# A four-image scan, attention and expert kernel: other VectorE work is put between each tick's product and scan

## The chip, the cores and the metric

The kernel runs on one core of a Trainium2 chip. A core has five engines that run side by side and each take their instructions in the order in which the program issues them: TensorE (PE, matmuls into PSUM), VectorE (DVE), ScalarE (ACT), GpSimd (POOL) and SyncE (SP, which here only issues DMAs). They wait for one another through semaphores. The metric is the device time of one execution in microseconds (us). Before the change it is 3908.64 us, the median of three runs (3907.09 to 3909.1).

## The reference, cut to what matters

There are four images of 384 channels and 32 x 32 pixels, so 1024 positions, in fp32. Layer 0 is a selective scan in four directions behind a group norm, layer 1 is causal attention and a mixture of four experts.

```python
# layer 0: x = x + gelu(layernorm(scan(groupnorm(x))))
def _gn(v, G=32, eps=1e-5):
    g = v.reshape(B_, G, C_ // G, H_, W_)
    m = jnp.mean(g, axis=(2, 3, 4), keepdims=True)
    s = jnp.var(g, axis=(2, 3, 4), keepdims=True)
    return ((g - m) / jnp.sqrt(s + eps)).reshape(v.shape)
...
def step(h, inp):                       # for every direction k, channel d, state n (16)
    dtt, ut, bt, ct = inp
    dA = jnp.exp(dtt[..., None] * A)
    h = h * dA + (dtt * ut)[..., None] * bt[:, :, None, :]
    y = jnp.einsum('bkdn,bkn->bkd', h, ct)
    return (h, y)
...
# layer 1
t = t + softmax(causal(q k^T)) v        # q, k, v from layernorm(t)
scores = jnp.einsum('bsd,de->bse', x, gate_w) + gate_b
probs = jax.nn.softmax(scores, axis=-1)
topk_vals, topk_idx = jax.lax.top_k(probs, TOP_K)       # 2 of 4
masked = probs * mask
masked = masked / (jnp.sum(masked, axis=-1, keepdims=True) + 1e-09)
h = jax.nn.gelu(jnp.einsum('bsd,edh->ebsh', x, w1) + b1)
y = jnp.einsum('ebsh,ehd->ebsd', h, w2) + b2
out = jnp.einsum('bse,ebsd->bsd', masked, y)
```

## The kernel before

The program is written out by hand in ticks (the `while` loop from L1158, with the tick in `clock`). There are 768 scan units: 4 images x 3 channel blocks `m` x 4 directions `k` x 4 state groups `q` x 4 channel groups `j`; each has 128 partitions (32 channels x 4 states) and 1024 positions. Tick t issues, in this order:

1. `decay(t + 2)` on ACT: da = exp(dt x a) (L505), three buffers;
2. what was deferred to this tick (`due`);
3. `front(t)` on DVE: v = du x B (L512), into PSUM, one buffer; both inputs are in SBUF;
4. `back(t - 1)` on POOL: the product h x C (L525), made to wait for this tick's v (`order`), both inputs in SBUF;
5. what was deferred to the inner place of this tick (`inner`), and the generators that parked themselves (`unpark`);
6. `middle(t)` on DVE: the scan (L518);
7. after every fourth unit `row(t - 2)` on PE, which sums the states into y (L550); then the DMAs for later ticks (`fetch`);
8. one step of the preparation of the next image, and `go_on`: the side generators, then the main work in line (`waiting`).

So DVE work that is issued in place 2 stands ahead of v, in place 5 between v and the scan, and in place 8 behind the scan, ahead of the next tick's v. A generator yields `"wait", n` to sleep n ticks, `"pe", x` to charge x us of PE to its budget, and `"inner", 0` to be taken up in place 5 of the next tick. The budget is `pace[0]` per tick: PACE_A = 4.4 in an attention, PACE_E = 3.3 in the experts.

What goes on beside the scans:

- `preparation(b)` loads image b, does its group norm (L297 to L338), the projections (`project_x`, `project_dt`), and writes dt and du = dt x u to DRAM, from where they are spread over the states. `project_dt` multiplies du in place 8 (L395), in the tick in which it takes a slot for it.
- `evict` (L566) collects y of an image; `finish(b)` does the layernorm, gelu, and the addition of x (L707, place 2). Then `behind(b)` runs `attention` and `experts`. `layernorm` subtracts (L601) and scales (L649) in place 5 and takes the reciprocal (L633) in place 8. It serves three callers.
- In attention, `softmax` (L777) stands in place 5 and `normalise` (L791), one tick later, in place 2. `gates` (L868) is a chain of small DVE operations in place 8, with a tick between its parts.
- `experts` runs 8 steps (2 halves x 4 experts); each has 12 groups `ph` (L1027), 6 groups `fy` (L1052) and three `out_` on DVE in place 5 (L1061, L1064). Behind the last expert of a half, `store` (L997) sends the result out.

Eight shared SBUF slots (`slots`) hold weights, du, dt, squares and softmax rows in turn; four PSUM banks (`banks`) are shared likewise. One large buffer, tag `a0`, holds the normed input of an attention (`axn`, L715) and then the second input and the accumulator of the same image's experts (`fx1`, L1081): the next image's axn cannot be written until the last store of the experts has been read out.

## Time and profile before

| what | us |
|---|---|
| median of three runs | 3908.64 |
| the profiled execution | 3911.65 |
| its span in the profile | 3909.9 |
| PE busy, of the span | 3382.8 (87%) |
| DVE busy | 3096.5 (79%) |
| ACT busy | 1887.9 (48%) |
| POOL busy | 1809.5 (46%) |
| start of the first v | 49.26 |
| start of the last scan | 3235.30 |
| first matmul of the last attention (L737) | 3302.51 |

The profile is one execution, taken by the hardware. A group line of it reads: line, engine, operation, output<-inputs, shapes and count | busy us in total, mean ns of one | idle time of the engine just before them, and what ended most of it. A line of waits reads: who <- for whom: us in total, times, longest. A line in order of time reads: start, duration, engine, line, operation. An instruction that is held up after it has started shows as a long one, not as idle time. A busy PE is modelled, and is not PE at its peak. The engines in the order of their load in the stretch of the scans are DVE and PE, close together; behind the last scan DVE and POOL have little to do.

### The profile page before, as it was taken

Reading aid. Unit: us, or ns where it says so; the run is one execution under the profiler, and the core shown is the slowest. Engines: PE = TensorE matmul, PEld = TensorE weight load, DVE = VectorE, ACT = ScalarE, POOL = GpSimd, SP = SyncE. Lnnn points to the kernel's source line nnn. Section 1 sums busy time; section 2 is a strip of 40 time slices with the busy share of each in tenths; the row PEclk is TensorE's granted clock in tenths of the full one; section 3 lists DMA queues with packets and bytes.
Section 4 is the critical chain, followed back from the end, with each engine's and each line's share of the span. In section 5 each row is a group of like instructions: output and inputs, shape, how many; then the busy total and the mean of one; then the engine's idle time right before and its main releaser. Section 6 shows DMA issues by size and latency. Waiting matters only on the chain.

```text
span 3909.9 us, 32087 instructions
## 1 busy us (share of the span) xinstructions
PE 3382.8 (87%) x10623; PEld 1389.4 (36%) x10623; DVE 3096.5 (79%) x2258; ACT 1887.9 (48%) x1996; POOL 1809.5 (46%) x776
## 2 busy tenths in 40 slices
PE   4554655659899999978999999799999998999999
PEld 1100100015433334435433343354334334644444
DVE  6999999998999999979999899989999993110000
ACT  5442543446656656546656545555455453322121
POOL 2665666654555556535555566455566661000000
PEclk7665666679899999989999999899999999999999
DMA  5554545453576667535666666426566651132321
GB/s 192 203 183 148 197 147 188 162 189 127 191 239 208 236 223 241 184 112 190 223 211 214 212 218 213 162 105 227 179 214 213 222 187 44 61 90 82 96 82 55
DMA packets 406087, 671.85 MB, mean 172 GB/s; under 512 B 33265, under 2 KB 280353, under 8 KB 405921
## 3 DMA queue, kind: packets, MB, share of 16 engines
q1 hardware_dynamic: 399712, 669.41, 50.5%
q8 instruction: 84, 1.38, 0.1%
q10 hardware_dynamic: 6208, 0.39, 0.1%
q14 instruction: 83, 0.67, 0.1%
HBM read 597.75 MB, written 71.96 MB: 171 GB/s over the span
## 4 chain that ended last, share of the span: by engine, by line
DVE 49%; PE 38%; issue 5%; ACT 4%; DMA 2%; POOL 1%; DVEq 1%; SPq 0%; POOLq 0%; ACTq 0%
DVE h L518 29%; DVE v L512 15%; PE ph L1027 13%; PE fy L1052 12%; PE y L550 3%; PE ss L766 2%; PE pq L737 2%; PE pv L748 2%; PE po L832 1%; ACT da L505 1%; DVE fy L1061 1%; ACT ht L1016 1%; PE pxd L350 1%; DMA du<-dts 1%; DVE du L395 1%
## 5 line engine op out<-in xcount | busy, mean ns | idle before, releaser
L525 POOL TENSOR_TENSOR h<-h,bc 128x1024 f32<-128x1024 f32 x768 | 1808.4, 2355 | 1430.0 <-DVE v L512 1278.1
L518 DVE TENSOR_TENSOR_SCAN h<-da,v 128x1024 f32<-128x1024 f32 x768 | 1755.5, 2286 | 86.1 <-DVE v L512 1.5
L505 ACT ACTIVATE da<-dt,a 128x1024 f32<-128x1024 f32 x768 | 878.0, 1147 | 1232.3 <-DVE h L518 1171.7
L1027 PE MATMUL ph<-fx,w 128*128 128x512 f32 x2304 | 1027.5, 602 | 9.4 <-ACT ht L1012 3.8
L1052 PE MATMUL fy<-ht,w 128*128 128x512 f32 x2304 | 1015.8, 598 | 2.4 <-ACT dt L387 0.9
L512 DVE TENSOR_TENSOR v<-du,bc 128x1024 f32<-128x1024 f32 x768 | 947.2, 1233 | 38.5 <-DMA du<-dts 16.4
L550 PE MATMUL y<-h,sel 128*32 128x512 f32 x3072 | 703.7, 713 | 309.5 <-POOL h L525 295.3
L1027 PEld LDWEIGHTS ph<-fx,w 128*128 128x128 f32 x2304 | 434.8, 192 | 588.9 <-issue 530.7
L1052 PEld LDWEIGHTS fy<-ht,w 128*128 128x128 f32 x2304 | 435.5, 191 | 570.5 <-issue 551.7
L1012 ACT ACTIVATE ht<-ph,b1s 128x512 f32<-128x512 f32 x384 | 257.6, 679 | 453.0 <-PE ph L1027 452.5
L550 PEld LDWEIGHTS y<-h,sel 128*32 128x32 f32 x3072 | 118.3, 118 | 831.7 <-POOL h L525 579.2
L1061 DVE SCALAR_TENSOR_TENSOR fy<-fy,b2s,tw 128x512 f32<-128x512 f32 x96 | 72.3, 754 | 424.1 <-PE fy L1052 424.1
L1016 ACT ACTIVATE ht<-ht 128x3072 f32<-128x3072 f32 x64 | 176.9, 2764 | 0.8
L505 ACT ACT_TABLE_LOAD x110 | 141.1, 1283 | 14.4 <-DMA dt<-dts 12.5
L766 PE MATMUL ss<-axn,qt 128*128 128x512 f32 (+3 forms) x288 | 105.3, 512 | 7.4 <-ACT yb L844 5.8
L832 PE MATMUL po<-pt,vt 128*128 128x256 f32 x480 | 103.6, 363 | 6.7 <-ACT pt L728 6.7
L832 PEld LDWEIGHTS po<-pt,vt 128*128 128x128 f32 x480 | 91.9, 193 | 21.7 <-ACT pt L728 9.2
L780 DVE TENSOR_REDUCE nb<-ss 128x1 f32<-128x512 f32 (+3 forms) x48 | 26.2, 554 | 82.8 <-PE ss L771 64.6
L381 PE MATMUL pdt<-xd,wdt 12*128 12x512 f32 x184 | 61.5, 690 | 34.4 <-ACT xd L354 26.5
L766 PEld LDWEIGHTS ss<-axn,qt 128*128 128x128 f32 x288 | 52.3, 199 | 53.3 <-issue 36.5
L1064 DVE TENSOR_TENSOR fx<-fx,fy 128x512 f32<-128x512 f32 x96 | 65.9, 687 | 3.3
L1016 ACT ACT_TABLE_LOAD x50 | 64.2, 1283 | 0.9
(183 smaller groups left out, 1406.5 us busy)
## 6 DMA issues: line engine op xcount, KB each, us to landing
bc<-rows SPq DMA_DIRECT2D x384, 512.0 KB, 4.7
w<-in_w SPq DMA_DIRECT2D x384, 384.0 KB, 6.0
dt<-dts SPq DMA_DIRECT2D x192, 512.0 KB, 4.0
du<-dts SPq DMA_DIRECT2D x192, 512.0 KB, 6.1
dts<-dt SPq DMA_DIRECT2D x48, 512.0 KB, 4.9
dts<-du SPq DMA_DIRECT2D x48, 512.0 KB, 4.6
fx<-t2d SPq DMA_DIRECT2D x12, 768.0 KB, 6.0
tw<-mkd SPq DMA_DIRECT2D x32, 256.0 KB, 5.7
```

The lines of the kernel that those rows point to most:

```text
L505: nc.scalar.activation(u["da"], spread["dt4", n], AF.Exp, scale=a4[:, g, u["q"] : u["q"] + 1])
L512: return nc.vector.tensor_tensor(u["v"], spread["du4", n], spread["bc", n][:, 0, :], ALU.mult)
L518: nc.vector.tensor_tensor_scan(u["h"][:, ::step], u["da"][:, ::step], u["v"][:, ::step], 0.0, op0=ALU.mult, op1=ALU.add,)
L525: product = nc.gpsimd.tensor_tensor(h, h, spread["bc", n][:, 1, :], ALU.mult)
L550: nc.tensor.matmul(y, sel, h, start=first, stop=last, tile_position=(0, jj * DJ))
L766: nc.tensor.matmul(ps[:, : e - o], qt[:, c, i * P : (i + 1) * P], xn[:, c, o:e], start=(c == 0), stop=(c == M - 1 and e <= i * P),)
L832: nc.tensor.matmul(pv[:, o:], vt[:, j, m * P : (m + 1) * P], pts[step][j // 4][:, j % 4, o:], start=False, stop=(j == nj - 1),)
L1012: nc.scalar.activation(ht[:, f, :], ps, AF.Identity, bias=bias)
L1016: nc.scalar.activation(ht, ht, AF.Gelu)
L1027: nc.tensor.matmul(ps, tiles[n][:, c, (f % 2) * P : (f % 2 + 1) * P], xns[h][:, c, :], start=(c == 0), stop=(c == M - 1),)
L1052: nc.tensor.matmul(pss[m], tiles[n][:, f, :], hts[fh][:, f, :], start=(fh == 0 and f == 0), stop=(fh == 1 and f == FH - 1),)
L1061: nc.vector.scalar_tensor_tensor(ps, ps, b2s[:, e, m : m + 1], tw, ALU.add, ALU.mult)
```

## The change

What it does, part by part:

- `unpark` comes ahead of `back`, and `"inner", n` now parks for n ticks more. `both` holds the DVE instruction for which the product waits: v, or, in a tick that has one, the du multiplication or the addition of x.
- du, the addition of x, `normalise`, the reciprocal of `layernorm` and the parts of `gates` go to place 5. Where ACT makes the input (the reciprocal, the second part of `gates`, the first du of a pair), one tick later. The two stores of du move accordingly.
- The ranks of the four gates are counted by comparing all with all in four operations of 128 x 64 and a sum, instead of in a loop; `lower` breaks ties by index. It is set by four memsets at the start.
- The group norm of images 1 to 3 takes its sums on ACT (Identity and Square with an accumulator), into one slot.
- `layernorm` can make its output buffer late: in attention axn is taken only when the image before is stored.
- PACE_E is 3.4; the store of an expert's half comes 3 ticks behind the last `fy` instead of 4.

```diff
@@ -41,7 +41,7 @@
 BANKS = 4
 SLOTS = 8
 PACE_A = 4.4
-PACE_E = 3.3
+PACE_E = 3.4
 @with_exitstack
@@ -95,6 +95,7 @@
     clock = [-100]
     due = {}
     inner = {}
+    both = []
     def defer(ticks, f, where=due):
         where.setdefault(clock[0] + ticks, []).append(f)
@@ -200,6 +201,11 @@
     a4 = const.tile([P, K * NG, NQ], F32, tag="a4", name="a4")
     sel = const.tile([P, DJ], F32, tag="sel", name="sel")
+    lower = const.tile([P, E, E], F32, tag="lower", name="lower")
+    nc.vector.memset(lower, 0.0)
+    for e in range(1, E):
+        nc.vector.memset(lower[:, e, :e], 1.0)
     dump = const.tile([P, 1], F32, tag="dump", name="dump")
     nc.scalar.activation(a_raw, a_raw, AF.Exp)
     nc.scalar.activation(dump, eps, AF.Sqrt)
@@ -297,7 +303,25 @@
     def groupnorm(b, u):
         st = sm.tile([P, M, NH, 6], F32, tag="gn_st", name=f"gn_st_{b}")
         mv = sm.tile([P, M, 2], F32, tag="gn_mv", name=f"gn_mv_{b}")
-        for m in range(M):
+        mean_c = sm.tile([P, M], F32, tag="gn_mc", name=f"gn_mc_{b}")
+        if b > 0:
+            var_c = sm.tile([P, M], F32, tag="gn_vc", name=f"gn_vc_{b}")
+            sq = yield from slots.take(f"gn_sq_{b}", P, L)
+            for m in range(M):
+                nc.scalar.activation(
+                    sq, u[m], AF.Identity, scale=-1.0 / L, accum_out=mean_c[:, m : m + 1]
+                )
+                yield "wait", 1
+            for m in range(M):
+                nc.scalar.activation(
+                    sq, u[m], AF.Square, bias=mean_c[:, m : m + 1], accum_out=var_c[:, m : m + 1]
+                )
+                yield "wait", 1
+            slots.give(f"gn_sq_{b}")
+            yield "inner", 0
+            nc.vector.tensor_scalar_mul(mean_c, mean_c, -1.0)
+            nc.vector.tensor_scalar_mul(var_c, var_c, 1.0 / L)
+        for m in range(M) if b == 0 else ():
             for h in range(NH):
                 nc.vector.bn_stats(st[:, m, h, :], u[m][:, h * 512 : (h + 1) * 512])
             nc.vector.bn_aggr(mv[:, m, :], st[:, m].rearrange("p h s -> p (h s)"))
@@ -306,8 +330,8 @@
             yield "wait", 1
         if b == 0:
             nc.vector.tensor_scalar_mul(gback, pgb[:NGRP, :C], float(C // NGRP))
-        mean_c = sm.tile([P, M], F32, tag="gn_mc", name=f"gn_mc_{b}")
-        nc.vector.tensor_copy(mean_c, mv[:, :, 0])
+            var_c = mv[:, :, 1]
+            nc.vector.tensor_copy(mean_c, mv[:, :, 0])
         yield "wait", 1
         mean = sm.tile([P, M], F32, tag="gn_mean", name=f"gn_mean_{b}")
         ps = yield from over_group(mean_c, f"mean_{b}")
@@ -316,7 +340,7 @@
         dev = sm.tile([P, M], F32, tag="gn_dev", name=f"gn_dev_{b}")
         nc.vector.tensor_sub(dev, mean_c, mean)
         nc.vector.tensor_mul(dev, dev, dev)
-        nc.vector.tensor_add(dev, dev, mv[:, :, 1])
+        nc.vector.tensor_add(dev, dev, var_c)
         yield "wait", 1
         rstd = sm.tile([P, M], F32, tag="gn_rstd", name=f"gn_rstd_{b}")
         ps = yield from over_group(dev, f"var_{b}")
@@ -388,14 +412,22 @@
                     dts[i][:, bass.ts(h, 512)], pss[i], AF.Softplus, bias=dtb[:, k, m : m + 1]
                 )
                 banks.give(f"pdt_{b}_{k}_{m}_{h}")
-        yield "wait", 1
+        def store(k, du):
+            nc.sync.dma_start(dts_d[b, k][1, m * P : (m + 1) * P, :], du)
+            slots.give(f"dt_{b}_{k}_{m}", f"du_{b}_{k}_{m}")
+        last = ()
         for i, k in enumerate(ks):
             nc.sync.dma_start(dts_d[b, k][0, m * P : (m + 1) * P, :], dts[i])
             du = yield from slots.take(f"du_{b}_{k}_{m}", P, L)
-            nc.vector.tensor_mul(du, dts[i], v)
-            yield "wait", 1
-            nc.sync.dma_start(dts_d[b, k][1, m * P : (m + 1) * P, :], du)
-            slots.give(f"dt_{b}_{k}_{m}", f"du_{b}_{k}_{m}")
+            yield "inner", 1 - i
+            both[:] = [nc.vector.tensor_mul(du, dts[i], v)]
+            if last:
+                store(*last)
+            last = k, du
+        yield "wait", 1
+        store(*last)
         if pair == 1:
             slots.give(f"ut_{b}_{m}")
@@ -577,14 +609,14 @@
             waiting.append(behind(b))
-    def layernorm(dst, src, name, lag):
-        width = dst.shape[2]
+    def layernorm(dst, src, name, lag, b=0, into=None):
+        width = src.shape[2]
         n = width // 512
         mus = []
         for h in range(n):
@@ -595,6 +627,11 @@
                 )
             mus.append(mu)
             yield "pe", 2.6
+        if into is not None:
+            while b > 0 and b - 1 not in stored:
+                yield "wait", 1
+            dst = into()
         yield "inner", 0
         for h in range(n):
             s = bass.ts(h, 512)
@@ -629,7 +666,7 @@
             rs, var[:, : n * P].rearrange("p (h t) -> p h t", t=P), AF.Sqrt, bias=eps
         )
         banks.give(f"var_{name}")
-        yield "wait", 1
+        yield "inner", 1
         nc.vector.reciprocal(rs, rs)
         yield "wait", lag
         backs = []
@@ -651,6 +688,7 @@
                 ALU.mult,
             )
             banks.give(f"rb_{name}_{h}")
+        return dst
     def fold():
@@ -704,15 +742,14 @@
             )
             def add(m=m, xr=xrs[m]):
-                nc.vector.tensor_add(yb[:, m, :], xr, yb[:, m, :])
+                both[:] = [nc.vector.tensor_add(yb[:, m, :], xr, yb[:, m, :])]
                 slots.give(f"xr_{b}_{m}")
                 if m == M - 1:
                     finished.add(b)
-            defer(1 + m // 2, add)
+            defer(1 + m // 2, add, inner)
     def attention(b, yb, fx0):
-        xn = ap0.tile([P, M, L], F32, tag="a0", name=f"axn_{b}")
         gw_ = []
         for name, w in ((f"wg_{b}", g_d), (f"wv_{b}", wv.rearrange("(c p) d -> p c d", p=P))):
             ta = yield from slots.take(f"{name}a", P, 2, C)
@@ -720,7 +757,10 @@
             tb = yield from slots.take(f"{name}b", P, C)
             nc.sync.dma_start(tb, w[:, 2, :])
             gw_.append((ta[:, 0, :], ta[:, 1, :], tb))
-        yield from layernorm(xn, yb, f"at_{b}", 0)
+        xn = yield from layernorm(
+            None, yb, f"at_{b}", 0, b,
+            lambda: ap0.tile([P, M, L], F32, tag="a0", name=f"axn_{b}"),
+        )
         qt = htp.tile([P, M, L], F32, tag="ht", name=f"qt_{b}")
         vt = htp.tile([P, L // P, C], F32, tag="ht", name=f"vt_{b}")
@@ -786,7 +826,7 @@
                     accum_out=nb[:, 2 + n : 3 + n],
                 )
                 banks.give(f"ss_{b}_{i}_{o}")
-            defer(1, lambda: normalise(i, nb, len(ss)))
+            defer(1, lambda: normalise(i, nb, len(ss)), inner)
         def normalise(i, nb, n):
             wd = (i + 1) * P
@@ -876,7 +916,7 @@
                     start=(c == 0), stop=(c == M - 1),
                 )
         yield "pe", 5.0
-        yield "wait", 1
+        yield "inner", 0
         sc = sm.tile([P, 4, E], F32, tag="sc", name=f"sc_{name}")
         nc.vector.tensor_tensor(
             sc, pg[:, : 4 * E].rearrange("p (q e) -> p q e", e=E),
@@ -892,29 +932,23 @@
         nc.vector.tensor_reduce(red, sc, AX.X, ALU.max)
         nc.vector.tensor_tensor(sc, sc, over(red), ALU.subtract)
         nc.scalar.activation(sc, sc, AF.Exp)
-        yield "wait", 1
+        yield "inner", 1
         nc.vector.tensor_reduce(red, sc, AX.X, ALU.add)
         nc.vector.reciprocal(red, red)
         nc.vector.tensor_tensor(sc, sc, over(red), ALU.mult)
+        cmp = [one.tile([P, 4, E, E], F32, tag=f"cmp{i}", name=f"cmp{i}_{name}") for i in range(2)]
+        each = sc.unsqueeze(3).to_broadcast([P, 4, E, E])
+        other = sc.unsqueeze(2).to_broadcast([P, 4, E, E])
+        nc.vector.tensor_tensor(cmp[0], other, each, ALU.is_gt)
+        nc.vector.tensor_tensor(cmp[1], other, each, ALU.is_ge)
+        nc.vector.tensor_tensor(
+            cmp[1], cmp[1], lower.unsqueeze(1).to_broadcast([P, 4, E, E]), ALU.mult
+        )
+        nc.vector.tensor_tensor(cmp[0], cmp[0], cmp[1], ALU.max)
         cnt = sm.tile([P, 4, E], F32, tag="cnt", name=f"cnt_{name}")
-        cmp = sm.tile([P, 4, E], F32, tag="cmp", name=f"cmp_{name}")
-        nc.vector.memset(cnt, 0.0)
-        for d in range(E):
-            other = sc[:, :, d : d + 1]
-            if d > 0:
-                nc.vector.tensor_tensor(
-                    cmp[:, :, :d], other.to_broadcast([P, 4, d]), sc[:, :, :d], ALU.is_gt
-                )
-                nc.vector.tensor_add(cnt[:, :, :d], cnt[:, :, :d], cmp[:, :, :d])
-            if d < E - 1:
-                nc.vector.tensor_tensor(
-                    cmp[:, :, d + 1 :], other.to_broadcast([P, 4, E - 1 - d]),
-                    sc[:, :, d + 1 :], ALU.is_ge,
-                )
-                nc.vector.tensor_add(cnt[:, :, d + 1 :], cnt[:, :, d + 1 :], cmp[:, :, d + 1 :])
-            if d % 2:
-                yield "wait", 1
+        nc.vector.tensor_reduce(cnt, cmp[0], AX.X, ALU.add)
+        yield "inner", 0
         mk = sm.tile([P, 4, E], F32, tag="mk", name=f"mk_{name}")
         nc.vector.scalar_tensor_tensor(mk, cnt, 1.5, sc, ALU.is_lt, ALU.mult)
         nc.vector.tensor_reduce(red, mk, AX.X, ALU.add)
@@ -999,6 +1033,8 @@
             nc.sync.dma_start(out[b, :, o : o + 512].rearrange("(m p) l -> p m l", p=P), acc)
             if h + 1 < NH:
                 defer(4, lambda: load(h + 1))
+            else:
+                stored.add(b)
         load(0)
         for h, e in [(h, e) for h in range(NH) for e in range(E)]:
@@ -1067,9 +1103,10 @@
                     defer(2, out_, inner)
             if e == E - 1:
-                defer(4, lambda h=h: store(h))
+                defer(3, lambda h=h: store(h))
     pace = [PACE_E]
+    stored = set()
     def behind(b):
         while b not in finished:
@@ -1092,16 +1129,19 @@
     ended = []
     def unpark():
-        for g in parked[:]:
-            parked.remove(g)
+        for g, tick in parked[:]:
+            if tick > clock[0]:
+                continue
+            parked.remove((g, tick))
             try:
                 what, n = next(g)
             except StopIteration:
                 ended.append(g)
                 continue
             if what == "inner":
-                parked.append(g)
-            until[id(g)] = clock[0] + (n if what == "wait" else what == "inner")
+                parked.append((g, clock[0] + 1 + n))
+                n += 1
+            until[id(g)] = clock[0] + (0 if what == "pe" else n)
             if what == "pe":
                 spare[0] -= n
@@ -1118,8 +1158,8 @@
             if what == "pe":
                 budget -= n
             elif what == "inner":
-                parked.append(g)
-                until[id(g)] = clock[0] + 1
+                parked.append((g, clock[0] + 1 + n))
+                until[id(g)] = clock[0] + 1 + n
             elif what == "start":
                 started.append(1)
                 break
@@ -1164,11 +1204,12 @@
         done = None
         if t < NU:
             done = front(t)
-        if 1 <= t <= NU:
-            back(t - 1, done)
+        both[:] = [done]
         for f in inner.pop(t, []):
             f()
         unpark()
+        if 1 <= t <= NU:
+            back(t - 1, both[0])
         if t < NU:
             middle(t)
         if t >= 2 and t - 2 < NU and (t - 2) % NJ == NJ - 1:
```

## The prediction

> **What bounds the kernel now.** I read the busy shares and the slices first, then the groups by line with shapes kept apart, then the waits of each engine, and last the order of time on VectorE (DVE) and GpSimd (POOL) around single ticks. In the slices, DVE stands at nine tenths until slice 33 and falls to 1 after it, while PE stays full.
>
> ```profile
> PE   4554655659899999978999999799999998999999
> DVE  6999999998999999979999899989999993110000
> PEclk7665666679899999989999999899999999999999
> L525 POOL TENSOR_TENSOR h<-h,bc 128x1024 f32<-128x1024 f32 x768 | 1808.4, 2355 | 1430.0 <-DVE v L512 1278.1
> L518 DVE TENSOR_TENSOR_SCAN h<-da,v 128x1024 f32<-128x1024 f32 x768 | 1755.5, 2286 | 86.1 <-DVE v L512 1.5
> L512 DVE TENSOR_TENSOR v<-du,bc 128x1024 f32<-128x1024 f32 x768 | 947.2, 1233 | 38.5 <-DMA du<-dts 16.4
> ```
>
> One tick is one v (L512) and one scan (L518): 1.233 + 2.286 = 3.52 us, and the gaps inside it (86.1 + 38.5 us less the first 15 us, over 768 ticks) bring it to 3.66. The scans end at 3237.6 us, so a tick really takes (3237.6 - 49.3)/768 = 4.15 us. The 0.49 between is 0.4 of other DVE work and some 70 us in all of waits above 1 us. After 3237.6 come 672 us of attention and experts of the last image, in which PE is the bound. In between, PE works at nearly the same load, so a saving on DVE counts until PE overtakes it.
>
> The waits of DVE, and the groups of its small operations:
>
> ```profile
> DVE nb L780 <- PE ss L771: 64.6, 18, 31.3
> DVE du L395 <- PE ph L1027: 16.5, 3, 9.9
> DVE axn L601 <- DMA out<-fx: 14.3, 3, 9.4
> L302 DVE BATCH_NORM_STATS2 gn_st<-x 128x6 f32<-128x512 f32 x24 | 15.1, 673 | 3.6 <-DMA x<-in_x 3.6
> L782 DVE TENSOR_TENSOR nb<-nb 128x1 f32<-128x1 f32 x16 | 9.9, 619 | 0.5
> L794 DVE TENSOR_TENSOR nb<-nb 128x1 f32<-128x1 f32 x16 | 2.2, 139 | 5.4 <-ACT pr L784 5.4
> L893 DVE TENSOR_TENSOR sc<-sc,red 128x16 f32<-128x16 f32 x8 | 1.4, 175 | 0.3
> ```
>
> The reader should stop at L782 and L794: the same operation on one column, 619 against 139 ns. L782 stands between v and scan, L794 before v. In order of time, one tick:
>
> ```profile
> 955.67 1.25 DVE L512 TENSOR_TENSOR v<-du,bc 128x1024 f32<-128x1024 f32 x1
> 956.84 1.14 DVE L780 TENSOR_REDUCE nb<-ss 128x1 f32<-128x512 f32 x2
> 957.09 2.35 POOL L525 TENSOR_TENSOR h<-h,bc 128x1024 f32<-128x1024 f32 x1 [1.26 <-DVE v L512]
> 958.01 1.44 DVE L782 TENSOR_TENSOR nb<-nb 128x1 f32<-128x1 f32 x1
> ```
>
> L782 takes 1.44 us and ends at 959.45, POOL's product at 959.44: the tiny operation waited for the product to end, and it doesn't show as idle time. At 1795.64 and 2599.83 the ends again agree within 0.02.
>
> **The Trainium skill.** "SBUF — State Buffer", section "Who interferes with whom": a DVE instruction with two SBUF inputs and a GpSimd instruction that reads SBUF exclude one another, and the later one blocks until the first has finished; one SBUF input (the other in PSUM) doesn't contend; a tensor_scalar can take the second port too. The trace agrees: L782 above, while L1064 (one input in PSUM) takes 687 ns in the mean. "VectorE: DVE Perf Modes", section on the TRN2 errata: fp32 tensor_tensor takes (N+151)/0.96 ns; the trace has 175 for N=16 and 1233 for 1024, so it serves for N=64: 224 ns, an estimate. "TensorE: Matmul & The Clock Gate", Part 1: idle lowers PE's clock; here the granted clock was 0.59 in 1680 to 1700 us, where PE was busy for 5 of 20 us.
>
> **The change part by part** (times against the profiled execution: span 3909.9, with 1.75 around it 3911.65, 3.0 above the median of 3908.64). Which tick an instruction falls in I counted by following the generators.
>
> Group norm of images 1 to 3. Removed per image: 6 x 673 + 3 x 209 + 173 = 4.84 us of DVE. Added: two tensor_scalar of about 0.17. Net 4.5, three times 13.5 us, all in the scan phase. The new multiplications stand right behind v; the first starts before the product (which follows v's end by 0.17), the second may be locked out: 0 to 2.3 us each image; I take 3 us in all. ScalarE gets 6 passes of about 1.23 and 0.195 each for the accumulator (L784's read), 8.6 us an image over 16 ticks (60 us), in which it is 40 to 66% busy: hidden.
>
> Ranks in the gates. Removed: a memset (72), 6 comparisons (1023 together), 6 additions (1015): 2.11 us. Added: 4 operations of 224 and a reduction of the same: 1.12. Saved 0.99, in six gates before the scans end: 5.9 us. (Two more are in the tail, beside PE.)
>
> Gates moved between v and scan. Before, they stood behind the scan, where the product is over but for 0.1 us. Now three blocks per gates stand beside it. The product runs from 0.17 to 2.52 after v's end. First block: 0.16 + 0.17, then sc-red with two SBUF inputs, which waits 2.52 - 0.33 - 0.175 = 2.0. Second: 0.155 + 0.178, then the multiplication by 1/sum, 2.0. Third: mk slips in ahead of the product (0.22), then 0.17 + 0.17 + 0.18, then mk times red: 1.6. Together 5.6 us, times six 34. Ticks with a du ahead of the gates are spared, or doubly hit: I take 31; bounds 0 (the lock lets them through) and 40. The first block is also 2.4 us nearer to the gate matmuls: +2 us of waits on PE.
>
> normalise, reciprocals, xr additions moved. normalise is first behind v, so it is ahead of the lock; the reciprocals have one input; for du and the xr additions the product is now ordered behind them (`both`), as it was by their old place. Zero, bounds -3 (waits on ScalarE such as 1.65 us at L896 vanish) and +5; I take -2. A layernorm comes out one or two ticks later, where DVE has scans to do; PE pays with idle time.
>
> Late hold. L601 of image 1 sits in the same tick (400) as the store it waits for, and stalls 9.4; image 2: 2.4. With the change the stores fall in ticks 394 and 588, L601 in 401 and 593: both waits go, -11.8. What is late next: pq begins in tick 404 rather than 402, and DVE's first softmax comes 8 ticks after it as before, so the 10.1 us wait at L780 there stays.
>
> du later. du was multiplied in the tick in which its slot was taken, and waited for PE still reading the slot's last weights: 5.2, 1.4, 5.4, 9.9 us at 1082, 1367, 2011, 2158. Now it has one or two ticks (4 to 8 us) more. All 22 gone would be the bound below; 5 of it the other, since PE may lag further. I take -14. The preparation of image 2 also leaves image 0's attention (pxd from ticks 222 to 226 to 241 to 245): -4 of the L780 waits.
>
> PACE_E 3.3 to 3.4. PE per tick: 3.4 + 0.46 (8 y matmuls of 1.85 us together every 4 ticks) = 3.86; with the pdt matmuls (4 x 0.86 every 18 ticks) 4.05. DVE: 3.66 + 0.24 (three out_ of 1.44 in some 18 ticks) = 3.90, with du 4.05. PE comes level with DVE in ticks 242 to 345 and 436 to 510. With clock dips to 0.8 in some 20 us windows it falls behind: 0 to +15, I take +4; the lag is worked off in ticks 389 to 401, where PE now has little. Fewer leftovers of image 2 remain behind the last scan (one fy group of 5.2 us less), but the reciprocal of the layernorm is queued behind the last out_: tail -2. On SP the store merely moves up a tick.
>
> Sum: -13.5 + 3 - 5.9 + 31 + 2 - 2 - 11.8 - 14 - 4 + 4 - 2 = -13.2 us: 3911.65 becomes 3898, and the median 3908.6 becomes 3895.4.
>
> **Rivals.**
> A. The lock doesn't bite the gates, or only in part (POOL starts later than I think): without 31 + 3 the sum is -47, 3861. For it: the gates' operations are tiny. Against: L782. PE would then be nearest to the bound, so 3864 is likelier.
> B. Slower: the lock on the small operations at its full price (40 + 5), and PE, loaded to 4.05 a tick, stalls DVE as much as du did (only 5 of 22 gained, pace +15). -13.5 - 5.9 + 45 + 2 - 11.8 - 5 + 15 - 4 - 2 = +20: 3929. It decides from the point where lock and lag exceed the 56 us of gains. For it: du's waits show PE behind by 10 us in ticks 468 and 502. Against: in ticks 660 to 767, 3.90 us each, PE follows without one DVE wait.
> C. Gains and lock cancel: within 8 us of 3908.6.
>
> **How the numbers follow.** Forecast (about -13) 0.48, A 0.20, B 0.15, C 0.17. About 0.2% (7.8 us) is what a measurement of this kernel can tell from no change. The forecast's spread of some 10 us leaves a third of it within that bound, so faster 0.62, same 0.21, slower 0.17. The range, 3864 to 3922, takes in A's likelier end and most of B.
>
> **What would show it.** bn_stats left 6 times only; sc and mk operations (now lines 937 to 960) with means well over 175 ns, ending with a product, some 1.5 to 2 us each for three of them per gates; no wait of axn on out before the tail; du waiting under 10 us in all; ticks 626 to 767 longer than before by some 10 us in sum; the tail from the last scan near 670. I am wrong if those operations still take 175 ns (A), or if DVE's waits on ph, fy and y grow past 30 us (B).

## The result and the profile after

The changed kernel takes 3936.26 us (median of 4 runs, 3935.56 to 3939.26) against 3908.87 for the kernel before beside it: ratio 1.0072, interval 1.0054 to 1.0089. It is slower by 27 us, where 13 us faster had been forecast. The profiled execution has a span of 3933.8 us.

From the groups by line of the changed kernel, shapes kept apart (busy us, mean ns | idle before, releaser):

```profile
L544 DVE TENSOR_TENSOR v<-du,bc 128x1024 f32<-128x1024 f32 x768 | 955.5, 1244 | 55.8 <-DMA du<-dts 24.6 <-DMA bc<-rows 5.1
L822 DVE TENSOR_TENSOR nb<-nb 128x1 f32<-128x1 f32 x16 | 14.1, 883 | 0.6
L955 DVE TENSOR_SCALAR red<-red 128x4 f32<-128x4 f32 x8 | 13.7, 1718 | 0.3
L938 DVE TENSOR_TENSOR sc<-sc,red 128x16 f32<-128x16 f32 x8 | 12.8, 1600 | 0.3
L933 DVE TENSOR_TENSOR sc<-sc,red 128x16 f32<-128x16 f32 x8 | 12.1, 1517 | 0.3
L943 DVE TENSOR_TENSOR cmp<-sc 128x64 f32<-128x64 f32 x8 | 1.8, 226 | 0.3
L957 DVE TENSOR_TENSOR mk<-mk,red 128x16 f32<-128x16 f32 x8 | 1.4, 175 | 0.3
L323 DVE TENSOR_SCALAR gn_vc<-gn_vc 128x3 f32<-128x3 f32 x3 | 0.5, 162 | 0.0
```

The gates' three blocks hold one instruction each of 1.5 to 1.7 us in the mean, on 16 or 4 columns. In the third it isn't the multiplication (L957, 175 ns) but the tensor_scalar two places ahead of it (L955). The same in order of time (start, duration, engine, line), two ticks of the changed kernel:

```profile
1080.79 0.17 DVE L932 TENSOR_REDUCE red<-sc 128x4 f32<-128x16 f32 x1
1080.85 2.34 POOL L557 TENSOR_TENSOR h<-h,bc 128x1024 f32<-128x1024 f32 x1 [1.26 <-DVE sc L921]
1081.00 2.23 DVE L933 TENSOR_TENSOR sc<-sc,red 128x16 f32<-128x16 f32 x1
1083.15 2.27 DVE L550 TENSOR_TENSOR_SCAN h<-da,v 128x1024 f32<-128x1024 f32 x1
...
1901.72 2.36 POOL L557 TENSOR_TENSOR h<-h,bc 128x1024 f32<-128x1024 f32 x1 [6.50 <-DVE mk L953]
1901.86 2.24 DVE L955 TENSOR_SCALAR red<-red 128x4 f32<-128x4 f32 x1
1904.13 0.18 DVE L956 RECIPROCAL red<-red 128x4 f32<-128x4 f32 x1
```

POOL's product ends at 1083.19 and 1904.08, the held DVE instructions at 1083.23 and 1904.10: they end with it. This is what "held" means below: the instruction has started, but ends only with the product. A reduction (one input) isn't held: L932 starts just ahead of the product in most ticks, but at 1014.78 us one runs inside a product and takes the same 170 ns. The multiplication L957 comes when the product is over, since L955 was held until then, so its 175 ns say nothing of whether it could be held. The hold counts as busy, so no view of waits has it. Line by line against 175, 175 and 170 ns before, it comes to 34.5 us in the six gates of the scan phase; the prediction had 31.

The waits of DVE in the changed kernel (us in total, times, longest):

```profile
DVE nb L820 <- PE ss L811: 56.9, 17, 30.6
DVE v L544 <- DMA du<-dts: 24.6, 4, 14.5
DVE h L550 <- PE y L582: 17.6, 6, 7.0
DVE du L425 <- ACT dt L411: 15.8, 6, 6.9
DVE v L544 <- DMA bc<-rows: 5.1, 1, 5.1
DVE du L425 <- PE fy L1088: 4.5, 2, 2.7
DVE du L425 <- ACT ht L1052: 4.0, 2, 2.3
```

axn's wait for out is gone from the scan phase, and du's for PE ph (16.5). In their place stand du's on softplus (ACT dt, 2.0 before), the scan's on y (none before), and more of v's on du and bc (24.6 + 5.1 against 16.4; 14.5 of it is the first v). SP's queue in the changed kernel, in order of time, shows what stands ahead of the late loads:

```profile
1609.63 0.34 SPq L361 DMA_DIRECT2D xnd<-x  x1
1610.02 0.52 SPq L505 DMA_DIRECT2D dt<-dts  x1
1613.80 0.34 SPq L361 DMA_DIRECT2D xnd<-x  x1
...
1616.39 1.23 SPq L516 DMA_DIRECT2D bc<-rows  x2
```

The stores of image 3's normed input (L361) go out while DVE is in ticks 379 to 382, before in 353 and 354. Two of them wait for ACT, 8.6 us in sum, with loads behind them in the same queue. DVE's v then waits 5.12 us for bc at 1623.25 and 5.40 for du at 1632.30. That the one causes the other isn't shown (experiment 9).

Where the time went, by ticks (start of v to start of v, in order of time; us before, and the difference of four kernels from it; three of them are described below, the fastest is that of experiment 10):

| ticks | before | changed | changed, pace 3.3 | gates behind scan | fastest |
|---|---|---|---|---|---|
| 0-242 | 976.1 | -16.1 | -15.1 | -17.0 | -18.1 |
| 242-386 | 593.0 | +34.9 | +11.7 | +26.6 | +0.8 |
| 386-404 | 100.1 | -14.0 | -15.2 | -14.1 | -15.2 |
| 404-434 | 139.1 | +5.9 | +12.4 | +3.7 | +7.6 |
| 434-596 | 687.3 | +0.5 | -8.8 | -11.8 | -21.0 |
| 596-768 | 692.7 | +13.8 | +15.6 | +0.8 | -1.9 |
| tail behind the last scan | 672.3 | +0.1 | +15.5 | +2.4 | +8.2 |

The losses stand in two kinds of ticks. Where gates stand (242 to 260, 434 to 455, 626 to 660) the changed kernel is 13.5, 7.5 and 12.4 us longer, 33.4 in all, the size of the hold. The other is ticks 260 to 386 (experts of image 0, the preparation of images 2 and 3), 21.4 us longer. The tail did not change.

DVE has no more to do in ticks 260 to 386 than before. Busy times of that stretch in the kernel before, the changed one, and the changed one at pace 3.3 (stretch and its length, then busy us and instructions of PE, PEld, DVE, ACT, POOL, the granted clock of PE, the share of DMA and GB/s):

```profile
1111.23:1618.35 507.12, 498.20 (x1529) 199.89 (x1528) 485.06 (x321) 302.36 (x288) 297.04 (x126) 1.00 0.67 225
1107.47:1635.99 528.52, 521.49 (x1577) 208.44 (x1576) 484.78 (x316) 324.15 (x315) 297.02 (x126) 0.99 0.66 223
1106.21:1612.81 506.60, 498.68 (x1525) 198.68 (x1524) 484.50 (x316) 319.36 (x311) 297.04 (x126) 0.99 0.68 230
```

DVE is busy for 485 us in all three. PE, whose busy time is modelled, is busy for 98 or 99% of the stretch in all three, before the change too. Its busy time grows by 23 us in the changed kernel, from 3.95 to 4.14 us a tick, where the prediction had put PE and DVE level at 4.05; at pace 3.3 it is back. What DVE waits in this stretch (26.9 us instead of 3.7) it waits mostly at du for ACT and at v for the loads of du and bc.

### The profile page after: what moved, and what is told of

Its sections match the earlier page's. It is cut to its first block, busy times and chain, and to the rows that moved or that the text cites. A ratio compares the mean times of both kernels' runs of the same rounds, so it can differ in the third digit from the quotient of the medians.

```text
span 3933.8 us, 32033 instructions
## 1 busy us (share of the span) xinstructions
PE 3397.8 (86%) x10623; PEld 1393.2 (35%) x10623; DVE 3124.3 (79%) x2174; ACT 1909.6 (49%) x2031; POOL 1809.0 (46%) x776
## 4 chain that ended last, share of the span: by engine, by line
PE 49%; DVE 38%; issue 4%; ACT 4%; DMA 3%; SPq 0%; DVEq 0%; POOL 0%; POOLq 0%; ACTq 0%
DVE h L550 23%; PE ph L1063 19%; PE fy L1088 19%; DVE v L544 12%; PE y L582 4%; PE pq L777 2%; PE pv L788 2%; PE ss L806 1%; PE po L872 1%; DMA du<-dts 1%; ACT da L537 1%; PE pxd L374 1%; ACT L411 0%; DMA w<-in_w 0%; DVE fy L1097 0%
## 5 line engine op out<-in xcount | busy, mean ns | idle before, releaser
L544 DVE TENSOR_TENSOR v<-du,bc 128x1024 f32<-128x1024 f32 x768 | 955.5, 1244 | 55.8 <-DMA du<-dts 24.6
L582 PE MATMUL y<-h,sel 128*32 128x512 f32 x3072 | 688.3, 706 | 305.8 <-POOL h L557 293.3
L806 PE MATMUL ss<-axn,qt 128*128 128x512 f32 (+3 forms) x288 | 111.5, 534 | 13.4 <-ACT yb L884 8.2
L405 PE MATMUL pdt<-xd,wdt 12*128 12x512 f32 x184 | 72.4, 775 | 45.3 <-ACT xd L378 26.4
L820 DVE TENSOR_REDUCE nb<-ss 128x1 f32<-128x512 f32 (+3 forms) x48 | 25.8, 552 | 70.2 <-PE ss L811 56.9
```

Source lines behind the costliest of these rows:

```text
L544: return nc.vector.tensor_tensor(u["v"], spread["du4", n], spread["bc", n][:, 0, :], ALU.mult)
L582: nc.tensor.matmul(y, sel, h, start=first, stop=last, tile_position=(0, jj * DJ))
L806: nc.tensor.matmul(ps[:, : e - o], qt[:, c, i * P : (i + 1) * P], xn[:, c, o:e], start=(c == 0), stop=(c == M - 1 and e <= i * P),)
```

## The experiments

Two theories stood at the start. L: the held operations of the gates are the loss. P: PE and ACT, loaded more by the pace of 3.4 and the group norm, are the bound, and what is taken from DVE comes back as waits. All medians stand beside the kernel before on the same chip, at 3909 to 3911 us; a difference between runs that stand beside different ones of these is good to a us or two.

**1. The gates behind the scan.** In the changed kernel, three lines of `gates`:

```diff
         yield "pe", 5.0
-        yield "inner", 0
+        yield "wait", 1
...
         nc.scalar.activation(sc, sc, AF.Exp)
-        yield "inner", 1
+        yield "wait", 1
...
         nc.vector.tensor_reduce(cnt, cmp[0], AX.X, ALU.add)
-        yield "inner", 0
+        yield "wait", 1
```

> The changed kernel with the three parts of the gates put back behind the scan (the new rank count is kept). Theory L (the port lock between VectorE's small two-input operations and GpSimd's product is the largest part of the loss): the three groups that stretch to 1.5 to 1.7 us fall back to 0.17, VectorE gets back 34 us, and the time goes from 3936 to 3902 +- 5. Rival P (PE, loaded to 3.4 per tick, is the bound and takes back what VectorE gains): at most 10 us less, 3926 or above, with VectorE's waits on PE and ScalarE grown instead.

3902.86 us (3899.16 to 3906.66), ratio 0.9981 (0.9972 to 0.999). The groups by line of this run:

```profile
L822 DVE TENSOR_TENSOR nb<-nb 128x1 f32<-128x1 f32 x16 | 13.1, 821 | 0.5
L933 DVE TENSOR_TENSOR sc<-sc,red 128x16 f32<-128x16 f32 x8 | 1.4, 174 | 0.3
L938 DVE TENSOR_TENSOR sc<-sc,red 128x16 f32<-128x16 f32 x8 | 1.4, 174 | 0.3
L955 DVE TENSOR_SCALAR red<-red 128x4 f32<-128x4 f32 x8 | 1.4, 169 | 0.3
```

33.4 us for three moved lines: L is shown. What is left of the change, though, is worth 7 us, where the prediction's terms without the gates' place (+31 and +2) come to 46.

**2. The same place in the kernel before**, with its rank loop in one block: gates between v and scan.

> The kernel before with one thing changed: the three parts of its gates (with the old loop of ranks) stand between v and scan. Theory L: six gates at 5.7 us of lock each make it 34 us slower, 3943 +- 6. Theory P: the place of the gates is worth less than 8 us, 3909 to 3917.

3943.5 us (3940.07 to 3946.82), ratio 1.0086 (1.0069 to 1.0103): 34 us, as L had it. The place costs the same in both kernels.

**3. The product ordered behind the held operation.** In the changed kernel the product waits for it, as it does for du:

```diff
-        nc.vector.tensor_tensor(sc, sc, over(red), ALU.subtract)
+        both[:] = [nc.vector.tensor_tensor(sc, sc, over(red), ALU.subtract)]
```

and so for the last comparison and the last product of `gates`.

> The changed kernel with the gates left between v and scan, but GpSimd's product ordered behind the last two-input operation of each of their parts, as is done for du. Theory L: the lock has nothing left to hold, the operations take 0.17 to 0.23 us, and the time is that of the gates behind the scan within 5 us (about 3902), since the product still ends with its scan. Theory P: 3926 or above. Should the place itself cost time (v of the next tick waits for the later product), this run is some 3 to 5 us slower than the one with the gates behind the scan.

3909.09 us (3904.31 to 3913.46), ratio 0.9996 (0.9989 to 1.0003). The three operations are back at 169 to 174 ns, so nothing is held, and yet it is 6 us dearer than the place behind the scan, a little more than the 3 to 5 that the expectation allowed for a later product.

**4. The pace.** The changed kernel with `PACE_E = 3.3`, and then the same with the gates behind the scan.

> The changed kernel with PACE_E back at 3.3. Theory P: the waits of the scan on y (17.6 us), of du on the softplus (16) and of v on bc and du loads (15) all stem from PE and ScalarE running late, and most of them go: 3936 to 3910 +- 8. Theory L: these waits shrink a little, and the tail gains no less than before; 3930 +- 6.

> The gates behind the scan and PACE_E back at 3.3. If pace costs what it cost with the gates beside the product (3936 to 3926), this is 3893 +- 4. If the two hide one another (a VectorE freed of the lock leaves PE more clearly the bound), pace is worth more here: 3885 or below. If pace only mattered because the lock delayed PE, nothing: 3903.

3925.78 us (ratio 1.0038, 1.0023 to 1.0053) and 3892.75 us (0.9953, 0.9937 to 0.997): the pace of 3.4 costs 10.5 and 10.1 us. By the marks set for the first run L was right (3930 +- 6) and P wrong (3910 +- 8); what P says of the pace is true, but it is the smaller part, and it adds to the price of the gates' place. The table shows what lies in it: 23 us less in ticks 242 to 386 and 9 less in 434 to 596, 6 more in 404 to 434 and 15 more in the tail. There, work of image 2 that the lower pace leaves over is done: 36 ph and 72 fy matmuls stand behind the last scan at 3.3, 64 fy at 3.4.

**5. The pace in the kernel before**, 3.4 for 3.3 and nothing else.

> The kernel before with one number changed: a pace of 3.4 instead of 3.3. In the changed kernel that number cost 10.5 us, where the prediction had 4 less 2 in the tail. Theory T (TensorE's load is the same in both kernels, so the higher pace makes it lag in any case): 8 to 14 us slower, 3917 to 3923, with more waits of du and of the scan on TensorE and ScalarE in ticks 242 to 345, and a shorter tail. Rival S (only together with the group norm sums on ScalarE does it stall): within 4 us of before.

3906.85 us, ratio 0.9995 (0.9987 to 1.0004): the sum is nothing, as the rival S had it, but not for its reason. Of the waits of DVE in this run:

```profile
DVE du L395 <- PE ph L1027: 15.5, 2, 8.9
DVE du L395 <- ACT dt L387: 11.3, 4, 5.1
DVE du L395 <- PE fy L1052: 8.9, 1, 8.9
```

du waits 41 us instead of 26, and ticks 242 to 386 are 15.8 us longer, as theory T had it. But at the higher pace the experts' store falls earlier, axn no longer waits for out (11.8 us before), and ticks 386 to 404 and 580 to 596 are 13.4 shorter. So the pace buys in the kernel before a part of what the late hold buys in the change, which has both; that they are paid only once together is an inference from these stretches, not a run.

**6. The late hold alone**, in the kernel before, with the store a tick earlier (the edits of `layernorm`, `attention` and `store` of the diff).

> The kernel before with the late hold of the attention's buffer alone, and the store of the experts' output one tick earlier. The normalisation of image 1 then stands one tick behind the store (ticks 400 and 399) instead of in the same one, that of image 2 two ticks behind it. If the hold is worth what the waits say: of 9.4 some 4 to 5 us go, and the 2.4 of image 2, so 3902 +-3 against 3908.9. Rival (the wait only moves to the next one): 3907 to 3911.

3907.36 us, ratio 0.9993 (0.9984 to 1.0001). No wait of axn on out is left in the scan phase, and the two stretches are 24.6 us shorter. Yet the median is only 2.3 us below the 3909.62 beside it: ticks 404 to 434 and 596 to 626 are 13 us longer, the tail is 678.1 instead of 672.3, with 26 ph and 72 fy matmuls behind the last scan instead of 69 fy. The rival, that the wait moves, was right.

**7. The group norm's sums, four times.** In the kernel before alone (sums on ACT, the multiplications behind the scan), and back on DVE in the kernels with gates behind the scan, at pace 3.4 and at a pace by image (`PACE_E = 3.3`, and 3.4 in the experts of image 2), against that kernel itself:

```diff
-        pace[0] = PACE_E
+        pace[0] = PACE_E if b < 2 else 3.4
```

> The kernel before with the group norm sums of images 1 to 3 on ScalarE and nothing else of the change (the two small multiplications behind the scan); VectorE does 13.5 us less. Theory (at pace 3.3 VectorE is the bound, as the 15.6 us in the two runs at that pace say): 10 to 15 us faster than before. Rival (ScalarE's 26 us and the preparation that starts 15 ticks later take it back in the kernel before): within 4 us of before.

> The gates behind the scan and the group norm sums of images 1 to 3 back on VectorE. VectorE has 13.5 us more to do: 3916 +- 4 if the move to ScalarE was a full gain; 3903 or below if the 26 us more on ScalarE (with the later softplus and the later stores behind it) cost as much as it gave.

> The changed kernel with the gates' three parts behind the scan and a pace of 3.3 for the experts of images 0 and 1, but 3.4 for image 2. At 3.3 throughout, the last scan ended 21.4 us earlier than at 3.4 (3202.6 against 3224.0 us), but the tail behind it was 688.6 us instead of 674.7, because seven experts of image 2 that 3.3 leaves over then stand ahead of image 3's attention. Theory (the pace of image 2 only decides what is left for the tail, that of images 0 and 1 is what stalls VectorE): scan end as at 3.3 within 4 us, tail 675, so 3880 +-4. Rival (the slow ticks of 242 to 404 come back wherever 3.4 is used, ticks 626 to 768 included): 3890 to 3900.

> The same, with the group norm sums of images 1 to 3 back on VectorE (13.5 us more VectorE work, 26 us less on ScalarE). At pace 3.4 that move was worth nothing (3901.9 against 3902.9). Theory N (at 3.4 TensorE was the bound where the sums stood, so VectorE time was worth nothing there; at 3.3 it is the bound again): 10 to 14 us slower than the run with the sums on ScalarE. Rival S (ScalarE's load itself makes the softplus and the du late, whatever the pace): within 4 us of it, or faster.

| the sums on | DVE | ACT | gain |
|---|---|---|---|
| kernel before, 3.3 | 3909.03 | 3908.36 (ratio 0.9999, 0.9992 to 1.0006) | 0.7 |
| gates behind the scan, 3.4 | 3901.88 (0.9975, 0.9965 to 0.9985) | 3902.86 | -1.0 |
| the same, pace by image | 3906.52 (0.9993, 0.9984 to 1.0001) | 3890.87 (0.9949, 0.9934 to 0.9963) | 15.6 |

The same 13.5 us of DVE time are worth nothing, nothing, and 15.6. In the second row ticks 260 to 386 are 529.5 us long with the sums on DVE and 527.6 with them on ACT, 507.1 before the change: what makes them long at pace 3.4 isn't ACT's load with the sums. The waits of du in the first run with the sums on ACT (in the kernel before) show where they went there:

```profile
DVE du L413 <- ACT dt L405: 17.1, 6, 7.4
DVE du L413 <- PE fy L1070: 16.5, 5, 6.7
DVE du L413 <- PE ph L1045: 8.5, 1, 8.5
```

42.1 us, 17 more than before: a DVE that is early waits at du for PE and ACT. Ticks 0 to 242 and 386 to 404 are 18.2 us shorter in it, 242 to 386 are 15.4 longer.

The 15.6 of the last row are not simply theory N's DVE time, though its number nearly fits. The two profiled executions are 11.5 us apart. Ticks 242 to 386 differ by 12.6 us, but DVE is busy there for only 3.5 us less; its waits on DMAs are 15.3 us with the sums on DVE and 3.9 with the sums on ACT. In the kernel with the sums on DVE:

```profile
DVE v L544 <- DMA bc<-rows: 7.7, 3, 6.3
DVE du L425 <- DMA dts<-dt: 4.8, 1, 4.8
```

Why these loads and stores come late there was not followed up. The pace by image itself missed its mark of 3880 and is level with 3.3 throughout (3892.75): its tail is 683.5 us, not 675, since PE comes to it with more of image 2's work undone, 14 ph and 72 fy matmuls against 64 fy at 3.4 throughout. (The "seven experts" of its expectation are wrong: at 3.3 the 36 ph and 72 fy named above are left over, and one of the 8 steps of an image has 72 of each.)

**8. du behind the scan again**, multiplied in the tick in which its slot is taken, first at pace 3.4 (from experiment 1), then at the pace by image (from experiment 10):

```diff
-            yield "inner", 1 - i
-            both[:] = [nc.vector.tensor_mul(du, dts[i], v)]
+            nc.vector.tensor_mul(du, dts[i], v)
+            yield "wait", 1
...
```

> The gates behind the scan and du multiplied as before (behind the scan, in the tick in which its slot is taken). Theory D1 (v grows to 1.37 us in the tick behind each du because the product, ordered behind du, ends after the scan): v's total falls by 7 us, and du's waits on ScalarE (18 us) become waits on PE of about 20 us: 3897 to 3903. Theory D2 (the later du was a gain, as forecast, that other losses hide): 3915 or more. Moreover the preparation ends earlier, so the stores of the normed image no longer fall in front of tick 384: if theory Q holds, another 10 us less, 3887 to 3893.

> The fastest of the versions so far (gates behind the scan, pace by image, minimum by a reduction; 3873.8 us) with du as the kernel before has it: multiplied in the tick in which its slot is taken, behind the scan. The prediction put the later du at a gain of 14 us; at pace 3.4 it measured 22. Theory D (the gain is the wait on TensorE and ScalarE that the later du spares, and is there at 3.3 as well): 10 to 20 us slower. Rival (at 3.3 TensorE is no longer late, and the v that is longer behind each later du costs as much): within 5 us.

3925.3 us (ratio 1.0035, 1.0022 to 1.0048) and 3891.53 us (0.9955, 0.994 to 0.997): 22.4 and 17.7 us slower than with the later du, as the theories D2 and D had it. The waits of the second:

```profile
DVE du L419 <- ACT dt L411: 22.3, 6, 8.0
DVE du L419 <- PE po L864: 3.2, 2, 2.5
DVE du L419 <- PE ph L1055: 2.8, 1, 2.8
DVE du L419 <- PE fy L1080: 1.2, 3, 0.6
```

29.5 us in these lines, against 7.1 on ACT and PE in the kernel it was made from. With the waits on DMAs, du waits 30.5 us in the scan phase against 12.7, which is the size of the loss. The later du is the part of the change that pays, and a little more than predicted (14).

**9. The stores of the normed input later**, the three of an image together, two ticks behind the last normalisation (from experiment 1).

> The gates behind the scan, PACE_E 3.4, and the three stores of a normed image (images 1 to 3) issued together two ticks behind the last normalisation instead of each right behind its own. Theory Q (these stores wait on ScalarE at the head of the DMA queue and hold back the loads for ticks 384 and 385): v's waits on bc and du loads lose some 10 us, 3893 +- 4. Rival: those waits come from the traffic itself (the loads land late whenever they are issued), no change, 3903 +- 3.

3917.68 us, ratio 1.0019 (1.0011 to 1.0026): 15 us slower than with the stores where they were, so both expectations failed. v waits less for bc (1.3 instead of 5.7) but du waits 27.5 for softplus instead of 15.0 and the scan 23.0 for y instead of 14.3. Why a store two ticks later costs that much was not followed up; it stays open what the stall on SP's queue is worth by itself.

**10. The softmax's minimum by a reduction** (from the pace by image): one input in SBUF instead of two.

```diff
-                nc.vector.tensor_tensor(nb[:, 0:1], nb[:, 0:1], nb[:, 1:2], ALU.min)
+                nc.vector.tensor_reduce(nb[:, 4:5], nb[:, 0:2], AX.X, ALU.min)
...
```

> The same as the first of these, with the softmax's minimum of two columns taken by a reduction over them (one input in SBUF) in place of an operation with two inputs in SBUF. That operation took 15.0 us over its 12 instances beside a product (1.25 us each, 0.16 in the tail). Lock theory: a reduction of 0.17 us each is not held, VectorE does 12 to 13 us less, and the part that is not eaten by the waits for TensorE's scores in the same ticks is gained: 5 to 13 us faster than the first run. Rival (any VectorE instruction that reads SBUF is held there, or the time is needed anyway for the scores): within 3 us.

3873.82 us (3869.04 to 3878.25), ratio 0.9908 (0.9891 to 0.9925): 17 us faster than the same without it, where 5 to 13 were expected, and the fastest of all, 0.9% under the kernel before. The group by line in this run (980 ns in the run without it):

```profile
L822 DVE TENSOR_REDUCE nb<-nb 128x1 f32<-128x2 f32 x16 | 2.5, 155 | 0.5
```

One tick of it in order of time:

```profile
929.45 0.87 DVE L820 TENSOR_REDUCE nb<-ss 128x1 f32<-128x512 f32 x2
930.35 0.15 DVE L822 TENSOR_REDUCE nb<-nb 128x1 f32<-128x2 f32 x1
930.42 2.28 DVE L550 TENSOR_TENSOR_SCAN h<-da,v 128x1024 f32<-128x1024 f32 x1
```

The scan starts right behind it, while the product that began at 929.64 us runs on. Of the 12 reductions in the scan phase 11 run inside a product, and each takes 154 to 156 ns. It is a hold that the kernel before has as well: the very instruction from which the prediction read the lock.

## Why the prediction was wrong, step by step

- **The lock on the gates (+31): right**, in mechanism and size: 34.5 in the profile, 33.4 when taken away. In the third block it caught a tensor_scalar and not the multiplication. The Trainium skill, "SBUF — State Buffer", section "Who interferes with whom", has the tensor_scalar among what can take the second port; L955 at 1718 ns against 169 behind the scan agrees. The lock on the group norm's multiplications (+3) did not come: L323 took 162 ns, since both multiplications began ahead of the product or with it.
- **What was left out of the sum.** L822 went from 619 to 883 ns (+4.2 us in all); it was 821 and 980 in other versions. The waits ahead of it did shrink, as forecast and by more: L820 waits 20.2 us on PE's scores in the scan phase instead of 32.1. But an L822 that comes earlier meets more of the product: 8 of 12 take over 1 us instead of 5, each ending with a product. So part of a wait that goes comes back as a hold; this is read from the trace and was not tried. v went from 1233 to 1244 ns (+8.3): where the product waits for a du, it ends about 0.3 us into the next v. In the run with du behind the scan at the pace by image, v was 6 us less in sum.
- **PACE_E (+4, tail -2): too small.** Measured 10.5 and 10.1. The prediction saw that PE comes level with DVE in ticks 242 to 345, and put the lag at 0 to 15; the price in ticks 242 to 386 is 23 us, against which the tail is 15 shorter than at 3.3. The tail of the change at 3.3 is longer than before's, by the 39 matmuls more that stand behind the last scan; the prediction had looked at the tail of the kernel before alone.
- **Late hold (-11.8): the wait went, the time did not.** Alone it is worth 2.3 us in the median, which its interval doesn't tell from nothing. Beside the pace of 3.4 it probably has less to remove, since the pace alone moves the store out of the way; the change without it was not tried.
- **Group norm on ACT (-13.5): right in DVE time, worth nothing at the pace of 3.4** (-1.0), nor alone (0.7). It is 15.6 at the pace by image, where the profiles show most of it as fewer waits on DMAs.
- **du later (-14): right in sign, small in size**: 17.7 and 22.4. (Of the four waits that it put down to PE, the one of 5.4 us at 2011 us stands in the trace as one on ACT's da.) One sign failed: du was to wait under 10 us in all and waits 24.9 in the changed kernel. It takes the pace and the sums on ACT together: with the gates behind the scan it is 23.0, at pace 3.3 11.2, and at 3.4 with the sums on DVE 5.2.

So the step that failed is the adding up. The prediction wrote that "a saving on DVE counts until PE overtakes it", saw PE come level, and then took DVE's savings at their full size and the lag at +4. Measured, the pace costs 10 and not +4 - 2, the sums on ACT give nothing at that pace and not 13.5 - 3, and the hold gives 2.3 and not 11.8. Without the two terms of the gates' place (+31 and +2) the prediction's terms made -46, and the kernel with the gates behind the scan had -7. By stretches, that kernel does gain 43 us in ticks 0 to 242, 386 to 404 and 434 to 596, but gives 27 back in 242 to 386, where PE was busy for 575.4 of 593.0 us before the change, and 7 elsewhere. By terms, of the 39 between, 8 are the pace, 11 the group norm with its lock, 10 the late hold and 5 the longer L822 and v (as far as du's figure doesn't hold them), less 8 for the du that gave more. These make 26, an estimate from the runs above, since they overlap; the other 13 stay open. The ranks (-5.9), the reciprocals and the L780 waits (-4) weren't tried apart.

Of the rivals, B (3929) named both lock and lag and was nearest in time, though its du and its price for the small operations were off, and its sign, waits on ph, fy and y above 30 us, did not come: fy and y make 22 us, and softplus on ACT another 16. The range ended at 3922, below B's own number, and the gains that B has to exceed are 53 us by the prediction's terms, not 56.

## What to carry to other kernels

When two engines are both near full, a wait of one for the other is often time that the other needs. Three parts of this change, each alone in the kernel before and each shortening some stretches by 13 to 25 us, moved the median by under 2.5 us, because the time came back where the two engines next had to meet. So look first for the place where they meet too early (here du, worth 18 to 22 us), and only then take work away. Before adding up savings, read the busy share of the other engine in each stretch; here it was 97% in ticks 242 to 386 before the change. Price a change of pace by the stretches that it loads, with the tail of the new order. Look in the busy time, not in the waits, for tiny operations with two SBUF inputs beside a long GpSimd instruction: a reduction over two columns did the same for 155 ns instead of 980.

## What the hardware showed that was not expected

- A product that starts late is paid by the next v as well: at 1077.24 us of the changed kernel it starts behind a du and runs 2.35 us, and the v issued at 1079.04 takes 1.64 us instead of 1.23. 51 of the v's of that kernel take over 1.3 us, 8.2 us more in sum; before it were 6.
- The reduction of experiment 10 took 13.2 us of busy time away and gave 17. The exponentials of the softmax start earlier too; whether the other 4 us come from there was not tried.
